# Four graph layers on 32 graphs: two issuing queues for the first adjacency matrix, and another order of all steps

## The chip, the cores and the metric

The kernel runs on one core of a Trainium2 chip. The metric is the device time of one launch, in microseconds (us). Three runs of the kernel before gave a median of 2910.88 us (2910.64 to 2910.99).

A core has engines that run side by side, each on its own instruction queue: TensorE (PE in the profile; its weight loads are PEld), VectorE (DVE), ScalarE (ACT), GpSimd (POOL) and SyncE (SP). Transfers are issued from the queues of SP, ACT and POOL.

## The reference

The inputs are x (32 graphs, 512 nodes, 256 features), adj (32, 512, 512) and a node mask, all in float32 but for the mask. Four layers follow each other; each is `x = layernorm(x + layer(x))`:

- Layer 0: `h = (1 + eps) x + adj @ x`, then `relu(h @ W1 + b1) @ W2 + b2`, with a hidden width of 512.
- Layer 1: graph attention with 4 heads: `e = leaky_relu(e_dst + e_src)` where `adj > 0.5`, softmax, times `x @ W`, plus a bias.
- Layer 2: attention with 8 heads of width 32: `softmax(q k' / sqrt(32) + log(adj + 1e-6)) v`, then an output projection with a bias.
- Layer 3: attention with one head: `softmax(mask((x W x') * adj)) x`.

## The kernel before

The graphs are independent. One graph is cut into several hundred steps by `graph(g)`; `prepare()` makes the steps for the weights. A step (`Step`) has a name, an engine, a planned duration, the steps it needs, the buffers it takes, and the instructions that it issues. Nodes come in 4 chunks of 128 partitions, features in 2.

Names of steps and lines that matter below:

- `la0i` to `la3i` (L670) issue the loads of the four 256 KB strips of a graph's adjacency matrix; `lxi` (L677) issues the load of x (512 KB). `at0` to `at3` (L695) transpose the strips on TensorE, `atd` (L701, DVE) and `ate` (L705, ACT) copy them out of PSUM, and `h0`, `h1` (L728) multiply x with the result into hT. `f` (L751) and `y` (L770) are the two dense products of layer 0.
- Layer 1: `v1` (L819), the row R that is sent through DRAM and broadcast, the elements `z` (L922 ACT, L933 DVE), products `o1` (L956), the sums `d1` (L993).
- Layer 2: `q`, `k` (L1078), `v2` (L1096), scores `s0` to `s7` (L1115), exponentials (L1128 ACT), the product with adj (L1137 DVE), values `n0` to `n7` (L1173), row sums `d2` (L1220), which GpSimd's adding transfers prepare (L1148, L1201), and the projection `p` (L1299).
- Layer 3: `i` (L1343), `t` (L1357), transposes `u` (L1396), `w` (L1411).
- Preparation: loads of eps, b1, the biases and two attention vectors go out on ACT's queue, the larger weights on SP's (all L348). `fmax`, `fm`, `fmt` (L530) and `fmb` (L540) find a bound on the scores.

TensorE works in four arrangements of its array. Most products use all of it. Scores use four tiles of 32 rows at a time (mode `row`), the values of layer 2 and all row sums use tiles of 32 columns (`c32`), those of layer 1 two tiles of 64 columns (`c64`).

The order in which the steps of all graphs are issued is worked out when the kernel is built, by `Plan.order`: it keeps a clock for each engine, takes the steps that could start within `ahead` of the earliest one, and issues the one with the lowest due time. A due time is made of the graph's turn times `period`, less the longest way from the step to the end of its graph, plus an offset for the step's name, plus `stay` times the price of a change of TensorE's arrangement:

```python
due = turn[g] * period - self.left[g][name] + moved[name] + stay * change
```

The prices stand in a table, `CHANGE`: 0.1 from the whole array to `row` or `c32`, 0.218 from `row` to anything else but itself, 0.13 from `c32` to the whole array, 0.12 from `c32` to `row`. The offsets `moved` come from a list of names and from disturbances that a random generator makes from seeds (`shifts`). `rush` moves the turns of the last three graphs forward. At most 6 graphs are open at once (`window`). All of this only sets the order in the queues; on the chip each instruction waits for what it needs.

Of the kernel before, what the change touches and what calls it, by code (L numbers as in the profile page):

```python
# [17 lines left out]
P = 128  # L18
# [28 lines left out]
class Plan:  # L47
# [31 lines left out]
    def step(self, name, eng, us, after=(), take=(), free=(), mode=""):  # L79


        def add(emit):
            steps = self.steps[-1]
            known = {**steps, **{f"^{n}": s for n, s in self.steps[0].items()}}
            assert name not in steps and all(a in known for a in after), (name, after)
            takes = []
            for b in take:
                kind, _, key = b.partition("=")
                key, _, rest = key.partition("/")
                takes.append((kind, key or kind, int(rest or 0)))  # L90
# [137 lines left out]
def fast_path(  # L228
# [23 lines left out]
    nc = tc.nc  # L252
# [47 lines left out]
    def blk(i):  # L300
# [257 lines left out]
    def graph(g):  # L560
# [3 lines left out]
        t = {"g": g}  # L564
# [7 lines left out]
        def strip(key, shape, name):  # L572
            return sb.tile(shape, F32, tag=f"D{slot[key]}", name=f"{name}_{g}")
# [88 lines left out]
        for c in range(NC):  # L662

            @step(
                f"la{c}i", "sp", 0.45, (f"la{c-1}i",) if c else (),
                take=(f"D=A0{c}/5",) if c else ("live", "L0", "D=A00/8"),
            )
            def _(c=c):
                t[f"A{c}"] = strip(f"A0{c}", [P, N], f"A{c}")
                nc.sync.dma_start(t[f"A{c}"], adj[g].rearrange("(c p) m -> p c m", p=P)[:, c, :])  # L670

            transfer(f"la{c}", 1.0 if g == 0 else 2.0, (f"la{c}i",), land=4.0 if g else 2.0)

# [1257 lines left out]
```

## Time and profile before

| | |
|---|---|
| median of three runs | 2910.88 us |
| the profiled execution: its time | 2910.6 us |
| its span, first to last instruction | 2908.8 us |
| mean granted TensorE clock | 0.998 |
| TensorE busy (15521 matmuls) | 2878.8 us, 99% |
| TensorE weight loads busy | 1655.2 us, 57% |
| DVE / ACT / POOL busy | 2256.4 / 1903.9 / 454.9 us |
| DMA, mean over the span | 148 GB/s |

The page gives the busy time of each engine and the chain of work that ended last. A line of a group or of the timeline names the kernel's line, the engine, the operation, the tiles written and read, and the shape; `32*128` is the part of the array in use (rows by columns). A line of the waits says which engine waited at which line for whom: in total, how often, and the longest. In the timeline the first two numbers are the start and the length in us, and what stands in brackets is the idle time ahead of it and what ended it.

### The profile page before, as it was taken

What the parts mean: (1) busy time and instruction counts of PE and PEld (TensorE: products, weight loads), DVE (VectorE), ACT (ScalarE), POOL (GpSimd) and SP (SyncE); (2) the same over time, 40 slices, a digit from 0 to 9 for tenths busy, and PEclk for the clock granted to TensorE, in tenths of its full rate; (3) what the DMA queues carried; (4) which work ended last, traced back from release to release, by engine and by line L of the source; (5) the groups of instructions that cost most, each with busy time, mean ns of one, the idle gap of its engine ahead of it and who ended that gap; (6) DMA issues with size and microseconds to landing.
All of it is one profiled execution on the core that took longest, in us unless ns stands there. A gap on an engine that the chain in (4) does not pass through costs nothing.

```text
span 2908.8 us, 42662 instructions
## 1 busy us (share of the span) xinstructions
PE 2878.8 (99%) x15521; PEld 1655.2 (57%) x15521; DVE 2256.4 (78%) x4389; ACT 1903.9 (65%) x3818; POOL 454.9 (16%) x494
## 2 busy tenths in 40 slices
PE   8989999999999999999999999999999999999998
PEld 6645555556555566555565555665555655556445
DVE  2786788777888777887778887778877788887975
ACT  3676666776656766667766567666667665676754
POOL 1111111111111111111111111111111111111110
PEclk9999999999999999999999999999999999999999
DMA  6367775567866567765678665677656786665851
GB/s 186 70 153 150 159 170 135 137 145 167 186 142 139 134 160 174 165 141 137 140 165 187 145 138 134 159 172 165 145 138 137 163 187 147 138 144 126 183 120 41
DMA packets 134879, 430.70 MB, mean 148 GB/s; under 512 B 13628, under 2 KB 53384, under 8 KB 102792
## 3 DMA queue, kind: packets, MB, share of 16 engines
q0 software_dynamic: 45568, 277.89, 49.2%
q1 hardware_dynamic: 88112, 149.75, 15.4%
q8 instruction: 125, 2.05, 0.3%
q14 instruction: 90, 0.74, 0.1%
q10 hardware_dynamic: 984, 0.28, 0.1%
HBM read 183.25 MB, written 17.08 MB: 69 GB/s over the span
## 4 chain that ended last, share of the span: by engine, by line
PE 95%; DMA 2%; ACT 1%; DVE 1%; issue 0%; POOL 0%; POOLq 0%; ACTq 0%; SPq 0%
PE s L1115 9%; PE o_ps L1173 8%; PE hT_ps L728 8%; PE o_ps L1411 8%; PE s L1357 8%; PE y_ps L770 8%; PE o_ps L956 7%; PE h1T_ps L751 7%; PE iT_ps L1343 4%; PE v_ps L819 4%; PE o2p_ps L1299 4%; PE kT_ps L1078 4%; PE qT_ps L1078 4%; PE v_ps L1096 4%; PE xT_t L1059 2%; PE eT_t L1396 2%
## 5 line engine op out<-in xcount | busy, mean ns | idle before, releaser
L1128 ACT ACTIVATE z<-s 128x512 f32<-128x512 f32 x1024 | 558.9, 609 | 131.4 <-PE s L1115 101.6
L1137 DVE SCALAR_TENSOR_TENSOR z<-AT,z 128x1024 f32<-128x1024 f32 x512 | 603.0, 1207 | 36.4 <-ACT z L1128 36.0
L933 DVE SCALAR_TENSOR_TENSOR z<-z,T,edge 128x512 f32<-128x512 f32 x512 | 363.7, 747 | 157.7 <-ACT z L922 156.9
L922 ACT ACTIVATE z<-R_bc,nT,S 128x512 f32<-128x512 f32 x512 | 395.5, 819 | 8.4 <-PE y_ps L770 3.0
L641 ACT ACTIVATE x<-x,shift,rstd 128x256 f32<-128x256 f32 x508 | 296.1, 609 | 152.0 <-DVE shift L631 152.0
L1148 POOL DMA_DIRECT2D z<-z x186 | 166.8, 903 | 1029.4 <-DVE nmax L1379 254.5
L623 POOL TENSOR_TENSOR rstd<-ve,nhalf 128x4 f32<-128x4 f32 (+1 forms) x131 | 153.5, 1172 | 978.2 <-DVE ve L617 953.8
L1115 PE MATMUL s<-qT,kT 32*128 32x512 f32 x2048 | 287.4, 633 | 1.0 <-ACT kT L1084 1.0
L1173 PE MATMUL o_ps<-z,v 128*32 128x512 f32 x2048 | 267.4, 602 | 1.8 <-DVE z L1137 1.7
L956 PE MATMUL o_ps<-z,v 128*64 128x512 f32 x1024 | 240.5, 601 | 2.1 <-DVE y L1028 2.1
L983 DVE TENSOR_TENSOR z<-z 128x1024 f32<-128x1024 f32 (+1 forms) x256 | 231.4, 952 | 13.0 <-PE o_ps L956 12.9
L1411 PE MATMUL o_ps<-x,eT 128*128 128x256 f32 x1024 | 239.3, 382 | 0.7 <-ACT eT L1401 0.7
L751 PE MATMUL h1T_ps<-hT,w_sb 128*128 128x512 f32 x512 | 230.4, 593 | 0.0
L1357 PE MATMUL s<-xT,iT 128*128 128x512 f32 x512 | 226.6, 594 | 0.7 <-ACT z L1128 0.7
L770 PE MATMUL y_ps<-w_sb,h1T 128*128 128x256 f32 x1024 | 226.7, 379 | 0.0
L1263 DVE RECIPROCAL rdT<-rdT 128x256 f32<-128x256 f32 x128 | 219.1, 1731 | 2.1 <-ACT rdT L1256 2.0
L600 DVE BATCH_NORM_STATS2 st<-x 128x6 f32<-128x256 f32 x508 | 211.0, 415 | 7.5
L1411 PEld LDWEIGHTS o_ps<-x,eT 128*128 128x128 f32 x1024 | 187.5, 190 | 46.3 <-ACT z L1387 21.0
L728 PE MATMUL hT_ps<-AT,x 128*128 128x384 f32 (+2 forms) x768 | 210.2, 383 | 0.0
L770 PEld LDWEIGHTS y_ps<-w_sb,h1T 128*128 128x128 f32 x1024 | 194.1, 190 | 27.9 <-issue 0.8
L1115 PEld LDWEIGHTS s<-qT,kT 32*128 32x128 f32 x2048 | 86.0, 183 | 166.0 <-ACT z L1128 118.8
L825 ACT COPY v<-v_ps 128x264 f32<-128x264 f32 x128 | 47.9, 376 | 183.7 <-PE v_ps L819 183.2
(155 smaller groups left out, 4241.3 us busy)
## 6 DMA issues: line engine op xcount, KB each, us to landing
z<-z POOLq DMA_DIRECT2D x186, 1024.0 KB, 8.5
A<-in_adj_dram SPq DMA_DIRECT2D x256, 256.0 KB
x<-biases POOLq DMA_DIRECT2D x96, 512.0 KB, 7.1
R_bc<-R_dram SPq DMA_DIRECT2D x32, 1024.0 KB
z<-z POOLq DMA_DIRECT2D x62, 512.0 KB, 8.7
x<-in_x_dram SPq DMA_DIRECT2D x32, 512.0 KB
out_dram<-x SPq DMA_DIRECT2D x31, 512.0 KB
nm<-in_nodemask_dram SPq DMA_DIRECT2D x32, 256.0 KB
```

The source lines that it names most:

```text
L728: nc.tensor.matmul(ph[:, cols], t["x"][:, m, blk(d)], moving, start=(k == 0), stop=(k == len(parts) - 1),)
L751: nc.tensor.matmul(ph, w1_sb[:, d, blk(f)], t["hT"][:, d, :], start=(d == 0), stop=(d == DC - 1))
L770: nc.tensor.matmul(py[:, j, :], t["h1T"][:, f, blk(2 * c2 + j)], w2_sb[:, f, :], start=(f == 0), stop=(f == HC - 1),)
L922: nc.scalar.activation(t[f"e{h}"][:, c, :], t["Rbc"][:, h, :], AF.Relu, bias=t["nT"][:, h, c : c + 1], scale=t["S"][:, h, c : c + 1],)
L933: nc.vector.scalar_tensor_tensor(z, z, t["T"][:, h, c : c + 1], t["edge"][:, c, :], op0=ALU.add, op1=ALU.mult)
L956: nc.tensor.matmul(po[j * F1 : (j + 1) * F1, :], t["v"][:, c, h * F1 : (h + 1) * F1], t[f"e{h}"][:, c, :], start=(c == 0), stop=(c == NC - 1),
L1115: nc.tensor.matmul(pk, t["k"][hs, o, blk(c)], t["q"][hs, o, :], start=True, stop=True)
L1128: nc.scalar.activation(t[f"E{k}"][:, j, :], t[f"ps{k}{j}"], AF.Exp, scale=QSCALE)
L1137: nc.vector.scalar_tensor_tensor(z, t["AT"][:, c, None, :].to_broadcast([P, 2, N]), ADJ_EPS, z, op0=ALU.add, op1=ALU.mult,)
L1173: nc.tensor.matmul(t[f"n{o}"][32 * j : 32 * j + 32, :], t["v2"][:, c, o * P + F2 * j : o * P + F2 * (j + 1)], t[f"E{k}"][:, j, :], start=( ...
L1357: nc.tensor.matmul(pt, t["iT"][:, d, blk(c)], t["xT3"][:, d, :], start=(d == 0), stop=(d == DC - 1),)
L1411: nc.tensor.matmul(py, t[f"eT{c}"][:, blk(m)], t["x"][:, m, :], start=(m == 0), stop=(m == NC - 1),)
```

## The change

For graph 0 alone, the loads of strips 1 and 3 are issued by ACT's queue, those of strips 0 and 2 by SP's as before. And the arguments of the plan are others: `stay` is 80 where it was 165, there are 14 seeds of disturbances where there were 8 (the first two are the same), the last three turns are moved by 1.7, 1.0 and 0.0 where it was 2.0, 1.1 and 0.1, and nearly all of the some 320 offsets of step names are different. The planner itself, the steps and what each step computes stay as they are.

```diff
             @step(
-                f"la{c}i", "sp", 0.45, (f"la{c-1}i",) if c else (),
+                f"la{c}i", "act" if g == 0 and c % 2 else "sp", 0.45, (f"la{c-1}i",) if c else (),
                 take=(f"D=A0{c}/5",) if c else ("live", "L0", "D=A00/8"),
             )
             def _(c=c):
                 t[f"A{c}"] = strip(f"A0{c}", [P, N], f"A{c}")
-                nc.sync.dma_start(t[f"A{c}"], adj[g].rearrange("(c p) m -> p c m", p=P)[:, c, :])
+
+                (nc.scalar if g == 0 and c % 2 else nc.sync).dma_start(
+                    t[f"A{c}"], adj[g].rearrange("(c p) m -> p c m", p=P)[:, c, :]
+                )
...
     with tc.manual_schedule():
-        plan.run([(24, 0.1, 6, 165.0, ((959604, 5.0), (114893, 5.0), (451585, 5.0), (104136, 2.0), (561761, 2.0), (241046, 2.0), (593942, 2.0), (984585, 2.0)), (2.0, 1.1, 0.1), (('R', 0.5), ('Re', -5.0),
...
-('la0.q', -74.0), ('la0i', -35.5), ('la1.q', -166.5), ('la1i', -58.5), ('la2.q', -21.5), ('la2i', 3.0), ('la3.q', -48.0), ('la3i', 4.0),
...
-('lx.q', -17.5), ('lxi', 9.0),
...
+        plan.run([(24, 0.1, 6, 80.0, ((959604, 5.0), (114893, 5.0), (428442, 5.0), (827982, 2.0), (379309, 5.0), (168251, 5.0), (904211, 5.0), (197558, 5.0), (201498, 2.0), (728276, 2.0), (358280, 2.0), (281265, 2.0), (22270, 2.0), (235352, 2.0)), (1.7, 1.0, 0.0), (('R', -7.5), ('Re', 3.0),
...
+('la0.q', 6.0), ('la0i', -1.0), ('la1.q', 9.0), ('la1i', 55.5), ('la2.q', -7.0), ('la3.q', 10.0), ('la3i', -2.0),
...
+('lx.q', 1.5), ('lxi', 2.0),
...
```

More of the change, by code (lines that the diff above doesn't have):

```diff
@@ L1458, in fast_path @@
     with tc.manual_schedule():
-        plan.run([(24, 0.1, 6, 165.0, ((959604, 5.0), (114893, 5.0), (451585, 5.0), (104136, 2.0), (561761, 2.0), (241046, 2.0), (593942, 2.0), (984585, 2.0)), (2.0, 1.1, 0.1), (('R', 0.5), ('Re', -5.0), ('Rl.q', 20.0), ('Rli', -15.0), ('Rs.q', 3.0), ('Rsi', 6.5), ('Rt', -62.0), ('ST', -37.5), ('ab', 6.0), ('as00', 6.5), ('as01', 6.0), ('as10', 0.5), ('as11', -1.0), ('as20', -27.0), ('as30', -86.5), ('as31', -18.5), ('at0', 3.0), ('at1', 2.0), ('at2', 9.5), ('at3', 6.0), ('atd0', -20.0), ('atd1', 0.5), ('atd2', -30.0), ('atd3', -21.0), ('ate0', 6.5), ('ate1', -13.0), ('ate2', 16.5), ('ate3', 19.0), ('cd1', 29.5), ('cd2', 17.0), ('cd3', 1.0), ('cd5', 39.5), ('cd6', 15.0), ('cd7', 33.5), ('cq1', -4.0), ('cq2', -78.0), ('cq3', 15.0), ('cq5', -20.0), ('cq6', -20.5), ('cq7', 2.0), ('d1', -25.0), ('de', 9.5), ('dev1.0', 27.0), ('dev2.0', 24.5), ('dev3.0', 12.5), ('dev4.0', 55.0), ('dt', 5.5), ('e00', 7.0), ('e01', -4.0), ('e02', 7.0), ('e03', 18.0), ('e10', 3.5), ('e11', 68.5), ('e12', -4.0), ('e13', 7.5), ('e20', 11.0), ('e21', -9.0), ('e22', 3.0), ('e23', -7.5), ('e30', -4.0), ('e31', -8.0), ('e32', 15.0), ('e33', 34.5), ('e40', -1.0), ('e41', -6.5), ('e42', 7.0), ('e43', -41.0), ('e50', 3.0), ('e51', 11.5), ('e52', 30.5), ('e53', 55.5), ('e60', 2.0), ('e61', -31.5), ('e62', 22.0), ('e63', 7.5), ('e70', 5.0), ('e71', 42.0), ('e72', 8.5), ('ed0', 32.0), ('ed1', -5.0), ('ed2', 72.0), ('f0', 19.0), ('f2', -0.5), ('f3', 8.0), ('fd0', 35.5), ('fd1', 41.0), ('fe0', -14.5), ('fe1', -1.0), ('fe2', -8.0), ('fe3', -4.0), ('fq0', -10.5), ('fq1', -10.0), ('h0', 19.0), ('h1', -8.0), ('he0', 2.5), ('he1', -14.0), ('hsb.q', 37.5), ('hsl', 7.0), ('i0', 6.0), ('i1', 7.0), ('ie0', -3.5), ('ie1', -1.0), ('k0', 2.0), ('k1', 18.5), ('ke0', 63.0), ('ke1', 2.0), ('la0.q', -74.0), ('la0i', -35.5), ('la1.q', -166.5), ('la1i', -58.5), ('la2.q', -21.5), ('la2i', 3.0), ('la3.q', -48.0), ('la3i', 4.0), ('lb0.q', -17.5), ('lb0i', -18.5), ('lb1.q', -2.0), ('lb1i', -15.5), ('lb2i', 6.0), ('lb3.q', -40.5), ('lb3i', -20.5), ('ldn.q', -0.5), ('ldni', 3.0), ('lx.q', -17.5), ('lxi', 9.0), ('m00', 2.5), ('m01', 9.0), ('m10', -16.0), ('m11', 12.5), ('m20', 6.5), ('m21', 0.5), ('m30', 4.5), ('m31', -4.5), ('m40', 13.0), ('m41', -31.5), ('m60', -24.0), ('m61', 42.5), ('m70', -1.0), ('m71', 19.5), ('n0', -2.0), ('n1', -31.0), ('n2', -6.5), ('n3', 6.0), ('n4', -3.5), ('n5', -12.0), ('n6', -12.5), ('n7', 32.5), ('nd0', 17.0), ('nd1', 32.0), ('no0', 0.5), ('no1', 9.5), ('node', 27.5), ('o100', 1.0), ('o101', 5.5), ('o110', 6.0), ('o111', 7.0), ('oe0', 23.5), ('oe1', 11.5), ('out0.q', 3.0), ('p0', 35.5), ('p1', 10.5), ('q0', 1.5), ('q1', -87.5), ('qe0', -27.0), ('qe1', -14.0), ('r10', 2.5), ('r11', 7.0), ('r12', 13.0), ('r13', -22.0), ('r20', 87.0), ('r21', 2.0), ('r22', -12.0), ('r23', 10.0), ('r30', 99.5), ('r31', -41.0), ('r33', 24.5), ('r40', -2.0), ('r41', -8.0), ('r42', -66.5), ('r43', 53.5), ('rc00', 5.0), ('rc10', 6.0), ('rc11', 6.5), ('rd1', -21.5), ('rd30', -68.5), ('rd31', 15.0), ('rd32', -5.5), ('rd33', -67.5), ('s0', 4.0), ('s1', -6.5), ('s2', -9.5), ('s3', -41.5), ('s4', -18.5), ('s5', -17.0), ('s6', -18.0), ('s7', -42.0), ('sh1.0', -1.0), ('sh2.0', 92.5), ('sh3.0', 59.0), ('sh4.0', -0.5), ('st10', -13.5), ('st11', 5.0), ('st12', -1.5), ('st13', 40.5), ('st20', -15.5), ('st21', 139.0), ('st22', 13.0), ('st23', 55.5), ('st30', 6.5), ('st31', 36.0), ('st32', 24.0), ('st33', -2.5), ('st40', -22.0), ('st41', 26.0), ('st42', -3.5), ('st43', 96.0), ('t0', 10.5), ('t1', -1.0), ('t2', -14.5), ('t3', -8.5), ('ta0', 27.0), ('ta1', 15.0), ('ta2', -3.5), ('ta3', -2.0), ('tb0', 4.5), ('tb1', -5.5), ('tb2', 4.0), ('tb3', -29.0), ('te0', -17.0), ('te1', -19.5), ('te2', 26.0), ('te3', -3.5), ('u0', -0.5), ('u1', -26.0), ('u2', 6.5), ('u3', 1.0), ('ue0', 17.0), ('ue1', 26.5), ('ue2', 30.5), ('ue3', -1.0), ('v10', 9.5), ('v11', -37.5), ('v12', 2.5), ('v13', -11.5), ('v20', 2.0), ('v21', -1.0), ('v22', -5.0), ('v23', 2.0), ('va1.0', 6.0), ('va2.0', 9.5), ('va3.0', 9.0), ('va4.0', 34.5), ('ve10', -5.5), ('ve11', -25.0), ('ve12', 9.5), ('ve13', -25.5), ('ve20', -1.5), ('ve21', 14.5), ('ve22', -6.0), ('ve23', -6.0), ('w0', 9.0), ('w1', 5.0), ('w2', 9.5), ('w3', -4.0), ('wx0', -29.5), ('wx2', 2.0), ('wx3', 21.5), ('x10', 1.0), ('x11', 1.0), ('x30', 1.0), ('x31', -10.0), ('xd1', -14.5), ('xd2', -5.0), ('xd3', -0.5), ('xe10', 4.0), ('xe11', -0.5), ('xe20', -3.0), ('xe21', -19.0), ('xe30', -23.5), ('xq1', -16.5), ('xq3', -45.0), ('xsi', -6.0), ('xt10', -46.5), ('xt11', -4.0), ('xt20', -6.0), ('xt30', -6.5), ('xt31', -5.5), ('y0', 9.5), ('y1', -4.0), ('yd00', -12.0), ('yd01', 59.5), ('yd10', 11.5), ('yd11', 88.0), ('yn0', -131.5), ('yn1', 9.0), ('yn2', -131.5), ('yn3', 17.5), ('yt0', 9.0), ('yt1', -21.5), ('yt2', -16.0), ('yt3', -18.0), ('z00', 13.5), ('z02', 104.5), ('z03', -3.0), ('z10', -4.5), ('z11', 12.0), ('z12', 3.0), ('z13', -2.0), ('z20', 22.0), ('z22', -11.5), ('z23', -6.5), ('z30', -2.0), ('z31', -39.0), ('z32', 21.5), ('z33', -7.0), ('zm00', -27.5), ('zm01', 56.5), ('zm10', -8.0), ('zm11', 21.5), ('zm20', 8.5), ('zm21', 0.5), ('zm30', 3.0), ('zm31', 28.5)))])
@@ new lines, in fast_path @@
+        plan.run([(24, 0.1, 6, 80.0, ((959604, 5.0), (114893, 5.0), (428442, 5.0), (827982, 2.0), (379309, 5.0), (168251, 5.0), (904211, 5.0), (197558, 5.0), (201498, 2.0), (728276, 2.0), (358280, 2.0), (281265, 2.0), (22270, 2.0), (235352, 2.0)), (1.7, 1.0, 0.0), (('R', -7.5), ('Re', 3.0), ('Rl.q', 1.0), ('Rli', -7.5), ('Rs.q', 12.5), ('Rsi', 40.0), ('Rt', -85.5), ('ST', -44.5), ('ab', 2.5), ('as00', -32.5), ('as01', -17.5), ('as10', -14.0), ('as11', -59.0), ('as20', -108.0), ('as21', -47.0), ('as30', -159.5), ('as31', -27.5), ('at0', -10.5), ('at1', -19.0), ('at2', -36.5), ('atd0', -28.5), ('atd1', -43.0), ('atd2', -17.5), ('atd3', -3.5), ('ate0', 22.5), ('ate1', 6.5), ('ate2', -9.5), ('ate3', 1.0), ('cd1', -3.5), ('cd2', -8.0), ('cd3', 13.5), ('cd5', -5.5), ('cd6', 2.5), ('cd7', 9.0), ('cq1', 47.5), ('cq2', 37.0), ('cq5', 34.0), ('cq6', -0.5), ('cq7', 24.5), ('d1', -79.5), ('d2', -2.0), ('de', -47.0), ('dev2.0', 5.5), ('dev3.0', -8.0), ('dev4.0', 19.5), ('dt', 7.0), ('e00', 7.0), ('e01', -6.0), ('e02', 36.5), ('e03', -22.5), ('e10', 5.0), ('e11', -18.0), ('e12', -15.5), ('e13', 11.0), ('e20', -37.0), ('e21', -14.5), ('e22', -0.5), ('e23', 48.5), ('e30', -6.0), ('e31', -1.5), ('e32', 7.5), ('e40', 2.0), ('e42', 5.0), ('e43', 2.0), ('e50', 1.0), ('e51', 7.0), ('e52', -5.0), ('e53', 0.5), ('e60', 24.0), ('e61', -9.5), ('e62', 1.0), ('e63', -3.0), ('e70', -4.0), ('e71', -3.0), ('e72', 8.0), ('e73', 4.0), ('ed0', 69.5), ('ed1', -14.5), ('ed2', -0.5), ('ed3', -5.5), ('f0', 36.5), ('f1', -11.0), ('f3', 2.0), ('fd0', 7.0), ('fd1', 6.0), ('fe0', -41.0), ('fe1', 11.0), ('fe2', -10.0), ('fe3', 3.0), ('fq0', 19.0), ('fq1', -19.5), ('h0', 15.0), ('h1', 4.5), ('he0', 7.0), ('he1', -0.5), ('hsb.q', 10.5), ('hsbi', -9.0), ('hsl', 1.0), ('i0', 5.5), ('i1', -29.0), ('ie0', 1.5), ('ie1', 10.0), ('k1', -2.5), ('ke0', 4.0), ('ke1', 47.5), ('la0.q', 6.0), ('la0i', -1.0), ('la1.q', 9.0), ('la1i', 55.5), ('la2.q', -7.0), ('la3.q', 10.0), ('la3i', -2.0), ('lb0.q', 2.5), ('lb0i', 10.5), ('lb1.q', -11.5), ('lb1i', 43.0), ('lb2.q', 50.0), ('lb2i', -5.0), ('lb3.q', -2.0), ('lb3i', 27.0), ('ldn.q', 19.5), ('ldni', 9.0), ('lx.q', 1.5), ('lxi', 2.0), ('m00', -11.0), ('m01', 2.0), ('m10', 26.5), ('m21', -22.5), ('m30', 1.5), ('m31', 12.5), ('m40', 14.0), ('m41', 12.5), ('m50', -14.0), ('m51', 3.0), ('m61', 52.5), ('m70', -5.0), ('m71', -2.5), ('n0', 19.0), ('n1', 8.0), ('n2', 6.5), ('n3', 12.5), ('n4', -6.0), ('n5', -8.5), ('n6', 3.0), ('n7', 1.0), ('nd0', -29.0), ('nd1', -25.5), ('no0', 23.5), ('no1', 10.0), ('node', -2.5), ('o100', 8.5), ('o101', -11.0), ('o110', 26.0), ('o111', 2.5), ('oe0', 5.5), ('oe1', 42.5), ('out0.q', 5.0), ('p0', 26.0), ('p1', 12.0), ('q0', -1.0), ('q1', 4.5), ('qe0', 9.0), ('qe1', -49.0), ('r10', -16.0), ('r11', -7.5), ('r12', 9.0), ('r13', 2.5), ('r20', 10.0), ('r21', -9.0), ('r22', 1.0), ('r23', 63.0), ('r30', 74.0), ('r31', -2.0), ('r32', 7.5), ('r33', 10.5), ('r40', 9.5), ('r41', 1.0), ('r42', 21.0), ('r43', 13.5), ('rc00', 10.0), ('rc01', -30.5), ('rc10', 30.0), ('rc11', -10.0), ('rd30', -34.5), ('rd31', 19.0), ('rd32', 2.5), ('rd33', -11.0), ('s0', 2.5), ('s1', 15.0), ('s4', -29.0), ('s5', -31.5), ('s6', -42.0), ('s7', -46.0), ('sh1.0', 0.5), ('sh2.0', 96.0), ('sh3.0', -10.0), ('sh4.0', 8.0), ('st10', 16.0), ('st11', 6.5), ('st12', 7.0), ('st13', 4.0), ('st20', -28.0), ('st21', 171.5), ('st22', 7.5), ('st23', 119.0), ('st30', 13.5), ('st31', 4.5), ('st32', 7.0), ('st40', 24.0), ('st41', -23.5), ('st42', 13.5), ('st43', -2.0), ('t0', 9.5), ('t1', -3.0), ('t2', 5.0), ('t3', 0.5), ('ta0', 46.0), ('ta1', 2.5), ('ta2', -14.0), ('ta3', -39.0), ('tb0', -7.0), ('tb1', -18.0), ('tb3', -28.5), ('te0', 1.0), ('te1', 6.5), ('te2', 12.0), ('te3', -1.0), ('u0', 18.0), ('u1', 8.0), ('u2', -39.0), ('u3', -18.0), ('ue0', -3.0), ('ue1', 3.0), ('ue2', 10.5), ('ue3', 1.0), ('v10', -11.5), ('v11', -26.5), ('v12', -7.0), ('v20', -1.5), ('v21', -18.0), ('v22', -12.5), ('v23', 1.0), ('va1.0', -1.0), ('va2.0', -5.0), ('va3.0', 22.5), ('va4.0', 16.0), ('ve10', -25.0), ('ve11', 2.0), ('ve12', 3.0), ('ve13', -5.0), ('ve20', 9.0), ('ve21', -2.0), ('ve22', 20.5), ('ve23', 7.0), ('w0', -5.5), ('w1', -1.0), ('w2', -7.0), ('w3', 11.0), ('wx0', -36.0), ('wx1', 3.5), ('wx2', -4.0), ('wx3', 8.0), ('x10', -21.0), ('x11', 13.5), ('x30', 19.5), ('x31', 2.0), ('xd1', -17.5), ('xd3', -1.0), ('xe10', -7.0), ('xe11', -1.0), ('xe20', -26.0), ('xe21', -2.0), ('xe30', -3.0), ('xe31', 4.0), ('xq1', -7.0), ('xq2', 61.5), ('xq3', 4.0), ('xs.q', 13.0), ('xt11', 13.5), ('xt21', -5.0), ('xt30', 1.0), ('xt31', -31.0), ('y0', 13.0), ('y1', -15.5), ('yd00', -3.5), ('yd01', 60.0), ('yd10', 30.0), ('yd11', 95.0), ('yn0', -150.5), ('yn1', -10.0), ('yn2', -241.0), ('yt0', 11.5), ('yt1', 0.5), ('yt2', -3.0), ('yt3', 12.0), ('z00', 23.0), ('z01', 34.0), ('z02', 60.0), ('z03', -7.0), ('z10', 2.5), ('z11', 8.0), ('z12', -21.0), ('z13', -42.0), ('z20', 21.0), ('z21', -3.0), ('z23', 0.5), ('z30', 3.0), ('z31', 6.0), ('z32', 43.0), ('z33', -2.5), ('zm00', -3.0), ('zm01', 109.5), ('zm10', 36.5), ('zm20', 44.5), ('zm21', -19.0), ('zm30', 1.0), ('zm31', 52.0)))])
```

## The prediction

> **What bounds the kernel now.** I read the page's busy times and its chain first, then the waits of TensorE, then TensorE's instructions in order of time for one graph in the middle, then the first 14 us.
>
> ```profile
> PE 2878.8 (99%) x15521; PEld 1655.2 (57%) x15521; DVE 2256.4 (78%) x4389; ACT 1903.9 (65%) x3818; POOL 454.9 (16%) x494
> PE 95%; DMA 2%; ACT 1%; DVE 1%; issue 0%; POOL 0%; POOLq 0%; ACTq 0%; SPq 0%
> ```
>
> TensorE is busy for 99% of the span and carries 95% of the chain that ended last. So only three things can move the time: the matmuls themselves (unchanged), what lies between them inside "busy" time, and TensorE's few idle stretches. The waits of TensorE alone:
>
> ```profile
> PE AT_t L695 <- DMA A<-in_adj_dram: 4.9, 1, 4.9
> PE hT_ps L728 <- DMA x<-in_x_dram: 4.5, 1, 4.5
> PE o_ps L956 <- DVE y L1028: 2.1, 1, 2.1
> PE o_ps L1173 <- DVE z L1137: 1.7, 4, 0.6
> PE fmb L540 <- DVE fm L535: 1.1, 1, 1.1
> ```
>
> Two are the first strips and the first x (9.4 us); the others are between 100 and 280 us. From 322 to 2371 us TensorE waits 0.2 us in all: every graph there takes 88.81 us, start of hT to start of hT. What a longer search can still find there is inside the busy time. One stretch of that period:
>
> ```profile
> 1089.83 1.14 PE L1115 MATMUL s<-qT,kT 32*128 32x512 f32 x8
> 1090.90 1.98 PE L1343 MATMUL iT_ps<-xT,w_sb 128*128 128x512 f32 x4
> 1092.82 1.14 PE L1115 MATMUL s<-qT,kT 32*128 32x512 f32 x8
> 1093.89 1.06 PE L1173 MATMUL o_ps<-z,v 128*32 128x512 f32 x8
> 1094.88 1.14 PE L1115 MATMUL s<-qT,kT 32*128 32x512 f32 x8
> ...
> 1100.87 7.03 PE L1357 MATMUL s<-xT,iT 128*128 128x512 f32 x16
> 1107.73 0.27 PE L1010 MATMUL d_t<-ident,dT 128*128 128x128 f32 x1
> ```
>
> Sixteen full-array matmuls take 1107.73-1100.87 = 6.86 us, 0.429 each. Four of iT should take 1.72 and take 1.92 before a tiling of another kind follows: +0.20. Eight score matmuls, four at a time in the 32-row tiling, should take 2x0.429 = 0.86 and take 1.07: +0.21. Eight of the 32-column tiling take 0.99: +0.13; the 64-column form gives +0.15 in the same way. I call a stretch in one tiling a run. The period has 22: 5 full-array, 7 of scores, 7 of 32 columns, 3 of 64. They cost 5x0.19 + 7x0.21 + 7x0.14 + 3x0.15 + 0.16 (a change inside the 32-column kind) = 4.0 us of 88.81; the matmuls alone need 84.8.
>
> Summed over the trace this way: 2734 us of matmuls, 125 us at the ends of 726 runs, 25.6 us of further stalls (20.8 of them between 100 and 280 us, where the pipeline fills), 4.9+9.0 us at the start, 0.8 in the last run and 9.9 after the last matmul: 2909, the span of 2908.8.
>
> **What the Trainium skill says.** "TensorEngine Tiling (Array Packing)", Key Properties: a change of tiling mode drains TensorE. The trace agrees: each change costs 0.13 to 0.21 us and inside a run there is nothing. "TensorE: Matmul & The Clock Gate", What's actually happening: after an idle window of some 3.4 us the array's clock falls to half. The trace agrees at 198 to 201.3 us, where the granted clock is 0.50 after the idle around fmt and fmb; eight matmuls lose about 1.7 us there. "DMA: Bandwidth & Descriptors", Issuing engines are not separate DMA queues: issuing from two engines saves only issue time. The trace bounds that: SP's four strip issues take 1.82 us.
>
> **The change, part by part.**
>
> *Strips 1 and 3 of graph 0 go from SP to ACT.* This removes 2 issues from SP, at 1.82/4 = 0.45 us each: 0.9 us. It adds 2 to ACT, whose own load issues take 0.33 to 1.19 us (median 0.42): 0.84 us. The start is bound by x, not by strips:
>
> ```profile
> 4.93 3.65 PE L695 MATMUL AT_t<-ident,A 128*128 128x128 f32 x16 [4.93 <-DMA A<-in_adj_dram]
> 5.88 0.37 SPq L677 DMA_DIRECT2D x<-in_x_dram  x1
> 13.04 0.77 PE L728 MATMUL hT_ps<-ATd,x 128*128 128x128 f32 x2 [4.47 <-DMA x<-in_x_dram]
> ```
>
> TensorE has transposed all strips at 8.58 and waits for x until 13.04. SP issues x only at 5.88, after w1 at 4.98, and both issues waited for earlier small loads (eps, b1) to land: the tenth and twelfth load wait for the second and fourth, so eight loads at most are in flight. If x takes the place that strip 1 leaves, it goes out near 1.2 us. Its 7.0 us from issue to landing then end at 8.2, and the bound passes to the strips. The new offsets work against them: la1i gets +55.5. Adding up the planner's durations, its due time without that is some 10 us before b1, 17 before the bias loads and 29 before a0 and a1, so +55.5 puts strip 1 behind all seven small loads on ACT. Those end at 7.1 in this trace. With 4.1 us from issue to landing (the first strip: 0.76 to 4.90), strips 1 and 3 land at about 11.3 and 11.7; 0.44 for a transpose and 0.54 for its copy give a first hT at 12.7. Best case (strips early, x at 8.2, copies at 8.4 to 11.1 moved up by 1): hT at 10, -3 us. Worst (ACT's eighth place waits for a landing that is itself late): +3. I take -1. Behind the two issues on ACT stand the table load (1.28) and the four AT copies (2.7 us), which end at 11.1 with 1.9 us to spare; without that cover the 0.84 us goes onto the start.
>
> *A new order for every step.* No computing instruction is added or removed; each queue is reordered, the loads on SP and the 344 adding transfers on POOL too. Three terms follow.
>
> Periodic part: from 322.2 to 2370.8 us are 23.07 periods. One pair of runs fewer per graph (scores and 32-column) saves 0.21+0.14 = 0.35 us, or 8.1 us; one more costs the same, or 0.41x23.07 = 9.5 where a full-array run is cut. Which way it goes can't be read from the list. The price of changes is weighted less (stay 165 becomes 80: leaving scores for the full array, priced 0.218, delays a due time by 17 us where it was 36), which speaks for more runs. For fewer speaks the room: 7 runs hold 8 score steps, and a pair of score steps already stands together once in the period. The planner sees this cost nearly right: its prices for the same period sum to 85.1+3.3 = 88.5 us against 88.81 measured. An order that is shorter for it should be shorter on TensorE. I take 20 runs per graph: -8.1. Bounds: 18 runs, -16; 24 runs, +9.5.
>
> What hides the reordering elsewhere is the slack of the other engines in a period: ACT 59 of 88.8 us busy, DVE 70, POOL 14, DMA engines 0.66. If that cover goes, a late DVE product appears as a TensorE wait. The largest seen after the start is 2.1 us; once per graph that would be 48 us, so I do not take the cover as certain.
>
> Filling, 100 to 280 us: stalls of 20.8 us over 58 runs, ended by DVE products, by the fmax-fm-fmb chain of the preparation, and by x normalised late. They happen once, and both orders meet the same latencies. Removing all gives -20.8; another bad crossing, say the 4.5 us around fmt and fmb again, +4.5. I take a tenth: -2.1.
>
> Draining: the last three graphs' due times are moved forward by 1.7, 1.0 and 0 times 24 us in place of 2.0, 1.1 and 0.1. Stalls there are 4.3 us, and 9.9 us lie after the last matmul. Between -4 and +4; I take 0.
>
> Sum: -1 - 8.1 - 2.1 + 0 = -11.2. Span 2908.8 - 11.2 = 2897.6; the profiled run was 2910.6, 1.8 outside the span, and the median is 0.3 above that: **2899.7 us**.
>
> **The rivals.**
> - *The orders are worth the same.* 22 runs again, the filling as before. For it: in the middle, the trace has nothing left but those 4.0 us a graph. Against it: 22 is far above the 14 or so that pairs of score and value steps would allow. With -1 at the start: 2910.
> - *Slower: more changes of tiling.* In the periodic part, the lighter price lets one more full-array step cut a score stretch per graph: 24 runs, +9.5, less 1 at the start: 2919. It decides from 0.25 us per graph on (5.8/23.07), less than one pair. For it: 165 to 80. Against: the planner still counts each change.
> - *Strip 1 comes late behind ACT's small loads.* The start loses 3 us and doesn't gain 1: 2903.7. For it: the +55.5 offset and the eight loads in flight. Against: x's own wait hides most of it. This is also the case in which the two queues don't do what they are for.
> - *A large gain.* 18 runs (-16.2) and half of the filling's stalls (-10.4), start -1: 2883.3. For it: 20.8 us of stalls stand in the trace. Against: they follow from few graphs being open.
>
> **How the numbers follow.** A measurement of this kernel can tell 0.2% (5.8 us) from no change. Forecast 0.38, large gain 0.13, late strip 0.05 (all faster by over 0.2%: 0.56); same 0.22; more changes 0.22. The range 2881 to 2920 takes in both ends of the run count and leaves out some 0.15, a worse start or broken cover above, a filling nearly free of stalls below. The likeliest case alone: 2893 to 2905.
>
> **What would show it.** Right: hT to hT near 88.46 us in the middle with 20 runs, hardly any TensorE wait there; fewer waits from 100 to 280 us; first hT at 12 us, no longer ended by x. Wrong: a period over 88.81, a TensorE wait that recurs each graph (DVE z or ACT xT), or a first hT after 13. If the period is as it was and the time is not, the ends decide, and my weights were misplaced.

## The result, and the profile after

The changed kernel takes 3039.1 us (median of four runs, 3031.3 to 3043.3) against 2910.9: a ratio of 1.0436, 95% interval 1.0414 to 1.0458. It is slower by 128 us, where 11 us less were forecast and 2920 was the upper end of the range.

From the page after, its busy times and its chain, by engine and by line:

```profile
PE 2915.9 (96%) x15521; PEld 1681.9 (55%) x15521; DVE 2239.7 (74%) x4389; ACT 1921.8 (63%) x3818; POOL 453.2 (15%) x494
PE 73%; DMA 18%; ACT 4%; DVE 3%; issue 1%; SPq 0%; POOL 0%; ACTq 0%; POOLq 0%; DVEq 0%
DMA R_dram<-R_rows 9%; PE s L1118 8%; PE s L1360 8%; PE o_ps L959 7%; PE o_ps L1176 7%; DMA R_bc<-R_dram 6%; PE y_ps L773 6%; PE kT_ps L1081 4%; PE iT_ps L1346 4%; PE v_ps L822 4%; PE h1T_ps L754 3%; PE o_ps L1414 3%; PE qT_ps L1081 3%; PE v_ps L1099 3%; PE hT_ps L731 2%; PE o2p_ps L1302 2%
```

Transfers carry 18% of the chain, where it was 2%, and two names that hardly stood on it before are among its longest: the 8 KB write of layer 1's row R to DRAM (9%), and its 1 MB broadcast load (6%). (The change shifts line numbers by 3.) The waits of TensorE:

```profile
PE kT_ps L1081 <- ACT xT L1066: 73.7, 18, 7.2
PE AT_t L698 <- DMA A<-in_adj_dram: 15.3, 3, 8.2
PE xT_t L1062 <- ACT x L641: 9.1, 19, 2.0
```

The first is a wait that the kernel before hardly had (0.4 us in all): k of layer 2 waits for a copy of xT by ACT, in 18 graphs, 4.1 us each. The time from the start of one graph's R transpose to the next shows where the 127.3 us of span come from. From graph 6 to graph 27 (21 periods) it was 88.81 us each before and is 93.61 on average now: +100.8. Up to graph 6 the kernel loses 15.1, after graph 27 it loses 11.4.

Periods without that wait take 88.56 us. They have 19 runs (stretches in one tiling) where there were 22, so the new order is better where the planner looked. One period with the wait, in the timeline of the changed kernel (SP's, GpSimd's and ACT's lines, and TensorE's wait):

```profile
1159.46 3.04 SPq L1330 DMA_DIRECT2D A<-in_adj_dram  x4
1161.33 0.86 POOL L1151 DMA_DIRECT2D z<-z  x1 [7.03 <-DVE z L1376]
1163.29 0.85 POOL L1151 DMA_DIRECT2D z<-z  x1 [1.09 <-ACT z L1390]
1163.82 1.17 POOL L1204 DMA_DIRECT2D z<-z  x1
1168.61 0.32 SPq L870 DMA_DIRECT2D R_dram<-R_rows  x1
...
1182.18 0.34 SPq L877 DMA_DIRECT2D R_bc<-R_dram  x1
1193.55 1.52 ACT L925 ACTIVATE z<-R_bc,nT,S 128x512 f32<-128x512 f32 x2 [12.33 <-DMA R_bc<-R_dram]
1194.97 1.05 ACT L1066 COPY xT<-xT_t 128x512 f32<-128x512 f32 x2
1195.59 3.78 PE L1081 MATMUL kT_ps<-xT,wkT 128*128 128x512 f32 x4 [4.37 <-ACT xT L1066]
```

Read it upwards. TensorE waits 4.4 us for xT. The two xT copies stand behind two z steps on ACT's queue, and ACT has waited 12.3 us for R_bc. R_bc could be issued only when R's own write had landed, 13.6 us after it went out. In the kernel before, the same place:

```profile
1199.30 2.79 SPq L1327 DMA_DIRECT2D A<-in_adj_dram  x3
1203.25 0.86 POOL L1148 DMA_DIRECT2D z<-z  x1 [10.58 <-DVE nmax L1379]
1203.79 1.17 POOL L1201 DMA_DIRECT2D z<-z  x1
1204.97 0.92 POOL L1148 DMA_DIRECT2D z<-z  x1
1209.25 1.99 SPq L867 DMA_DIRECT2D R_dram<-R_rows  x1
...
1217.65 0.34 SPq L874 DMA_DIRECT2D R_bc<-R_dram  x1
```

There the last strip of layer 3's adjacency matrix goes out before GpSimd's three adding transfers, and R's write lands in 8.4 us. In the changed order, the first adding transfer gets in ahead of the last strips. What the queues moved in the 4 us after R's write, first the changed kernel (1168.6 to 1172.6 us), then the one before (1209.25 to 1213.25):

```profile
q0 software_dynamic: 103, 0.76, 91.4%
q1 hardware_dynamic: 104, 0.19, 14.4%
```

```profile
q0 software_dynamic: 112, 0.77, 103.4%
```

q0 is GpSimd's queue, q1 that of SP. Before, nothing of q1 moved in these 4 us, not even R's own write; no strip was left ahead of it. Now q1 still holds strips, and they drain at 0.19 MB in 4 us beside the adding transfers' 0.76. The packet counts are equal, 103 and 104. This is as the Trainium skill has it in "DMA: Bandwidth & Descriptors", Queues, rings and completion order: each DMA engine goes round between the queues packet by packet. With packets of 7.4 KB on average on one side and 1.8 KB on the other, equal turns give the strips a fifth of the bytes. R's write stands behind them.

Over graphs 6 to 27, R's write to the issue of its load takes 8.2 us before and 13.1 now, and the first z after that load comes 16.2 us and 22.6 us after the write. ACT's wait for R_bc, from 497.8 to 2370 us, first before and then now:

```profile
ACT z L922 <- DMA R_bc<-R_dram: 0.7, 1, 0.7
ACT z L925 <- DMA R_bc<-R_dram: 202.9, 20, 13.9
```

Most of the waits also cost clock: at 15 of the 18, those of 2.4 us and more, TensorE's granted clock is 0.50 for 3.4 or 6.8 us, beginning during the wait or within 1.4 us after it. After the wait above, from the windows view (the third number from the end is the clock):

```profile
1195.60:1199.00 3.40, 3.40 (x4) 1.49 (x5) 2.17 (x8) 3.40 (x6) 0.00 (x0) 0.50 1.10 226
```

Four matmuls of kT take 3.78 us there, 1.88 without a wait ahead of them.

### The profile page after: what moved, and what is told of

It is laid out like the page before. It is cut to its first block, busy times and chain, and to the rows that moved or that the text cites. A ratio compares the mean times of both kernels' runs of the same rounds, so it can differ in the third digit from the quotient of the medians.

```text
span 3036.1 us, 42696 instructions
## 1 busy us (share of the span) xinstructions
PE 2915.9 (96%) x15521; PEld 1681.9 (55%) x15521; DVE 2239.7 (74%) x4389; ACT 1921.8 (63%) x3818; POOL 453.2 (15%) x494
## 4 chain that ended last, share of the span: by engine, by line
PE 73%; DMA 18%; ACT 4%; DVE 3%; issue 1%; SPq 0%; POOL 0%; ACTq 0%; POOLq 0%; DVEq 0%
DMA R_dram<-R_rows 9%; PE s L1118 8%; PE s L1360 8%; PE o_ps L959 7%; PE o_ps L1176 7%; DMA R_bc<-R_dram 6%; PE y_ps L773 6%; PE kT_ps L1081 4%; PE iT_ps L1346 4%; PE v_ps L822 4%; PE h1T_ps L754 3%; PE o_ps L1414 3%; PE qT_ps L1081 3%; PE v_ps L1099 3%; PE hT_ps L731 2%; PE o2p_ps L1302 2%
## 5 line engine op out<-in xcount | busy, mean ns | idle before, releaser
L1131 ACT ACTIVATE z<-s 128x512 f32<-128x512 f32 x1024 | 540.0, 610 | 97.2 <-PE s L1118 93.1
L925 ACT ACTIVATE z<-R_bc,nT,S 128x512 f32<-128x512 f32 x512 | 402.9, 818 | 248.9 <-DMA R_bc<-R_dram 245.2
L641 ACT ACTIVATE x<-x,shift,rstd 128x256 f32<-128x256 f32 x508 | 290.0, 614 | 161.3 <-DVE shift L631 161.3
L1176 PE MATMUL o_ps<-z,v 128*32 128x512 f32 x2048 | 259.0, 602 | 2.0 <-DVE z L1140 1.9
L1360 PE MATMUL s<-xT,iT 128*128 128x512 f32 x512 | 244.4, 605 | 0.0
L754 PE MATMUL h1T_ps<-hT,w_sb 128*128 128x512 f32 x512 | 238.4, 609 | 1.9 <-ACT hT L738 1.9
L986 DVE TENSOR_TENSOR z<-z 128x512 f32<-128x512 f32 (+1 forms) x256 | 231.1, 952 | 4.6 <-PE o_ps L959 4.6
L1081 PE MATMUL kT_ps<-xT,wkT 128*128 128x512 f32 x256 | 146.2, 700 | 74.1 <-ACT xT L1066 73.7
L902 DVE CUSTOM_DVE_ANT_0 xs_row<-xs_row,wgT 128x256 f32<-128x256 f32 x64 | 27.2, 425 | 216.0 <-DMA xs_row<-xs_dram 214.9
## 6 DMA issues: line engine op xcount, KB each, us to landing
z<-z POOLq DMA_DIRECT2D x62, 512.0 KB, 10.6
```

Of the source, the lines that this page charges most:

```text
L754: nc.tensor.matmul(ph, w1_sb[:, d, blk(f)], t["hT"][:, d, :], start=(d == 0), stop=(d == DC - 1))
L925: nc.scalar.activation(t[f"e{h}"][:, c, :], t["Rbc"][:, h, :], AF.Relu, bias=t["nT"][:, h, c : c + 1], scale=t["S"][:, h, c : c + 1],)
L1081: nc.tensor.matmul(pq, wT[n][:, d, blk(o)], t["xT2"][:, d, :], start=(d == 0), stop=(d == DC - 1))
L1131: nc.scalar.activation(t[f"E{k}"][:, j, :], t[f"ps{k}{j}"], AF.Exp, scale=QSCALE)
L1176: nc.tensor.matmul(t[f"n{o}"][32 * j : 32 * j + 32, :], t["v2"][:, c, o * P + F2 * j : o * P + F2 * (j + 1)], t[f"E{k}"][:, j, :], start=( ...
L1360: nc.tensor.matmul(pt, t["iT"][:, d, blk(c)], t["xT3"][:, d, :], start=(d == 0), stop=(d == DC - 1),)
```

## The experiments

Two parts were taken alone first. The theory: the loss is R's late round trip, which ACT's queue hands on to TensorE. Rivals: the start with its two queues; ACT's new order by itself; the adding transfers slowing every transfer alike. Each ratio is against runs of the kernel before that were made beside it (medians 2911.5 to 2912.0 us).

**The two queues alone.** The kernel before, in its order:

```diff
-                nc.sync.dma_start(t[f"A{c}"], adj[g]...)
+                (nc.scalar if g == 0 and c % 2 else nc.sync).dma_start(t[f"A{c}"], adj[g]...)
```

> The kernel before, in its own order, with strips 1 and 3 of graph 0 issued by ACT at the places that the order before gives them (strip 1 right after eps). Theory: the first part of the change is small by itself. The first hT waits for x, and x now goes out up to 0.9 us earlier: 2908 to 2912 us. Rival (the two queues are what costs): over 2920 us.

Measured: 2913.7 us, ratio 1.0005 (0.9996 to 1.0014), no difference that can be told, though just over the expected range. First hT came later and not earlier, at 14.1 us and not 13.0: x no longer ends the wait, strip 3 does. It went out on ACT at 9.1 us, behind bias loads.

**The order alone.** The changed kernel with all strips on SP:

```diff
-                f"la{c}i", "act" if g == 0 and c % 2 else "sp", 0.45, ...
+                f"la{c}i", "sp", 0.45, ...
```

> The changed kernel's order with all strips of graph 0 on SP again. Theory: the loss comes from the repeated stalls of the middle, so nearly all of it stays: 3025 to 3040 us, with the first hT some us earlier than 19.3. Rival (the start costs most): below 2950 us.

Measured: 3028.7 us, ratio 1.0386 (1.0339 to 1.0433). First hT at 15.5 us, TensorE's wait for xT 71.0 us in 17 graphs. The order makes nearly all of the loss; ACT's share in the strips adds some 4 us at the start.

**R's load without R's write.**

```diff
-                t["Rbc"].rearrange("p h n -> p (h n)"), row_bcast(t["Rdram"], H1 * N)
+                t["Rbc"].rearrange("p h n -> p (h n)"), row_bcast(biases.rearrange("k c d -> k (c d)")[0:1, :], H1 * N)
```

> The changed kernel, with the broadcast row R read from a DRAM row that is written once at the start, so that its load needn't wait for the landing of R's own 8 KB write (layer 1's R is left out of the result; all instructions stay). Theory (the round trip of R is late, ACT waits for it with the xT copies behind): ACT's wait for R_bc and TensorE's wait for xT go from 74 us to under 10, the middle period becomes 88.6 us: 2915 to 2935 us. Rival (ACT's order alone makes xT late): 3020 us or more.

Measured: 2922.6 us. The wait for xT no longer stands among TensorE's waits, and the middle takes 88.61 us on average. ACT's own order, with z ahead of xT, is the same in this run: it does no harm when R comes in time. ACT still waits for R_bc here, 96.3 us in 21 graphs, and the first z starts 17.1 us after R's write; that much TensorE bears.

**R's write from another queue.** The result stays whole here:

```diff
-            nc.sync.dma_start(t["Rdram"], t["Rr"][: H1 * NC, :])
+            nc.scalar.dma_start(t["Rdram"], t["Rr"][: H1 * NC, :])
```

> The changed kernel, with R's 8 KB write issued by ACT's queue in place of SP's, nothing else moved. Theory (the write stands in SP's ring behind strips that are still draining beside the adding transfers): from Rs to the issue of R_bc it takes 3 to 5 us and not 12.9, the stalls of xT shrink to under 15 us in all: 2915 to 2945 us. Rival (the adding transfers slow every transfer, whichever ring it is in): still 10 us or more, and over 3000 us.

Measured: 2925.5 us, ratio 1.0043 (1.0029 to 1.0057). Write to load takes 5.6 us on average (3 to 5 were expected), and z starts 16.3 us after the write, against 16.2 in the kernel before. TensorE's wait for xT in this run:

```profile
PE kT_ps L1081 <- ACT xT L1066: 1.6, 2, 1.4
```

One word in one line takes back 114 of the 128 us. The adding transfers run as in the changed kernel, so the rival that they alone make R this late is out: most of the lateness comes from standing behind the strips in SP's queue. They are not without effect. R's write took 8.2 us in the kernel before, with no strip ahead of it in the window shown above, and ACT still waits 92.3 us for R_bc in this run. The prediction took over that a second issuing engine saves only issue time; here a second queue saved 114 us, because what stood ahead of the write was left behind.

**Smaller adding transfers.** The changed kernel with a quarter of each row:

```diff
-  src, dst = (t[f"E{b}"].rearrange("p h n -> p (h n)") for b in (k, a))
+  src, dst = (t[f"E{b}"].rearrange("p h n -> p (h n)")[:, :N] for b in (k, a))
```

> The changed kernel, with GpSimd's adding transfers of the row sums cut to a quarter of each row (three quarters of the sums of layer 2 are left out; the same number of transfers). Theory (the strips drain slowly because of the adding transfers, and R behind them): Rs to R_bc takes under 5 us, hardly a stall of xT: 2910 to 2930 us. Rival (R is late by its own latency or by SP's order): still over 10 us, over 3000 us.

Measured: 2908.8 us, just below the expected range; middle 88.56 us, write to load 3.7 us, and ACT's wait for R_bc is gone. So both must come together for the loss: strips still queued ahead of R (without them, in the kernel before, 8.2 us and no loss), and adding transfers that take most of the engines' time beside them. What wasn't run is the new order with the last strips ahead of the adding transfers again.

**z behind the copies on ACT.** The changed kernel; in `run`, the order `out` is edited before its steps are issued (`xe20` and `xe21` are the two xT copies):

```diff
+        for g in range(6, 28):
+            i = max(k for k, e in enumerate(out) if e[0] == g - 1 and e[1] in ("xe20", "xe21"))
+            late = [e for e in out[:i] if e[0] == g and len(e[1]) == 3 and e[1][0] == "z"]
+            if [e[1] for e in late] != ["z10", "z30"]:
+                continue
+            out = [e for e in out[: i + 1] if e not in late] + late + out[i + 1 :]
```

> The changed kernel, with the first two z steps (z10, z30) of each graph in the middle moved behind the two xT copies on ACT's queue; R comes as late as before. Theory (ACT's queue carries R's lateness to TensorE): TensorE's wait for xT, 74 us, is gone, but the copies of h1T stand behind z31 and wait in its place, so a good part comes back there: 2950 to 3020 us. Rival (xT is late for another reason): no change, 3030 us or more.

Measured: 3058.9 us (two runs), no faster than the changed kernel. The waits of TensorE there:

```profile
PE kT_ps L1088 <- ACT xT L1073: 39.8, 10, 6.9
PE xT_t L1069 <- ACT x L648: 36.7, 35, 2.9
...
PE y_ps L780 <- ACT h1T L767: 8.0, 8, 1.3
```

The edit took hold in 13 of the 22 graphs. In the other nine, two stretches in the middle, four z steps stand ahead of xT, and the code leaves them alone. In the 13, TensorE's wait for xT is gone; the 39.8 us come from graphs that were not edited. But the 13 are no faster, 94.2 us per period where the same graphs took 93.6: waits for other ACT work take its place, for normalised x (up to 2.9 us) and h1T. By its time the run falls into the rival's range (3030 us or more); the waits speak against the rival, as xT is on time once no z stands ahead of it. That ACT carries the lateness is borne out; my size was not. Moving one consumer past a late producer moved the stall to the next one.

**A late R in the kernel before.** Twice written, and then three times, in its own order. The edit for two writes (`once` is another DRAM tile):

```diff
+            nc.sync.dma_start(once, t["Rr"][: H1 * NC, :])
-            nc.sync.dma_start(t["Rdram"], t["Rr"][: H1 * NC, :])
+            nc.sync.dma_start(t["Rdram"], once)
```

> The kernel before, with R's row written to DRAM twice in turn (first to another DRAM tile, then copied from there), so that its round trip is 4 to 8 us longer; the rest as before. Theory (both orders leave R a margin of 1 to 2 us, and the one before only happens to stay within it): the period rises by 2 to 6 us and the same waits for xT or h1T appear: 2960 to 3040 us. Rival (the order before tolerates a late R, the new order is what is fragile): 2911 to 2920 us.

Measured: 2924.1 us; z starts 18.0 us after the first write, 1.8 later than before, and the period rises by 0.08 us only. The expectation missed: two writes came to less than I had reckoned, and 1.8 us is still within what TensorE bears; the time falls between the ranges of theory and rival. Of the 11 us of span lost here, 6.2 are after graph 27.

> The kernel before, with R's row written three times in turn, so that z starts 21 to 22 us after the first write and not 16.2 (18.0 with two writes, where the period rose by 0.1 us only). Theory (both orders have the same shape there, and only the lateness of R tells them apart): the period rises by 3 to 5 us, with TensorE waiting for xT: 2990 to 3030 us. Rival (the order before tolerates a late R, which is why it was fast): under 2950 us.

Measured: 3131.1 us (two runs), ratio 1.0753 (1.0733 to 1.0774). z starts 24.7 us after the first write (I had reckoned with 21 to 22), and the period is 96.87 us, so the loss is larger than expected. From the waits of TensorE:

```profile
PE kT_ps L1082 <- ACT xT L1067: 137.8, 27, 8.1
```

The same instruction waits for the same copy. The order before shows no sign of being more robust than the new one: it bears 1.8 us of lateness, and at 8.5 us it loses 8.1 per graph. The loss per graph goes with the start of z after the write, whichever order it is: in the order before 16.2 us, no loss; 18.0, 0.1 us; 24.7, 8.1; in the new order, over its 88.56 us, 16.3 and 17.1, 0.05 us; 22.6, 5.05.

**The start.** Since strip 1 came late, three versions of the kernel before put graph 0's loads first. Strips 0 and 2 and x on SP, strips 1 and 3 first on ACT:

> The kernel before, with the four strips and x of graph 0 ahead of all other loads: strips 0 and 2 and then x on SP, strips 1 and 3 first on ACT. Theory (two queues help only if nothing stands ahead of the strips): first hT at 9 to 11 us and not 13.0, TensorE's waits at the start 5 us shorter: 2905 to 2909 us. Rival (the loads' bandwidth sets the start): first hT at 12 to 13 us, 2911 us.

Measured: 2911.9 us, ratio 1.0001 (0.9992 to 1.0010), the rival's number. The first hT matmul is at 8.6 us: x is early. But the AT copies stand on ACT behind loads of biases and vectors that wait to be issued, and TensorE stops again until 14.0 us. Then these loads behind the AT copies:

> The kernel before, with the strips and x of graph 0 first as in the run before it, and the loads of the biases and attention vectors behind the four AT copies on ACT's queue. Theory (in that run x had landed by 8.6 us, and only the AT copies, which stood behind waiting load issues on ACT, kept TensorE idle until 14.0): the whole hT runs from about 9 us, 4 to 5 us earlier than before: 2905 to 2908 us. Rival (another load, w1 or the biases, then comes late and takes it back): 2910 to 2914 us.

Measured: 2911.6 us, ratio 0.9999 (0.9991 to 1.0008). First hT at 10.6 us. Now the 0.5 KB load of eps, third on ACT, lands only at 9.1 us; the ATd additions need it and the copies wait for those. Then eps first:

> As the run that put the strips and x of graph 0 first and the loads of the biases and attention vectors behind the AT copies, but with eps as ACT's first load again. Theory (there the small eps load had slipped behind the strips, the ATd additions waited for it until 9.5 us, and the AT copies for those): the AT copies start at about 5.5 us, hT when x lands at 8 to 10 us: 2906 to 2909 us. Rival (the start of the kernel is worth nothing because a later wait takes it up): 2910 to 2913 us.

Measured: 2910.5 us against 2911.6, ratio 0.9998 (0.9990 to 1.0006). First hT at 8.9 us, 4.2 earlier than before; but graph 1's hT starts only 1.4 us earlier and the span is 1.0 us shorter, as the rival said. In this order the start can be won and is then given back within the filling, so the two queues are worth nothing there that can be measured.

**Both mended.** The new order, R's write on ACT, and the start with eps behind the strips:

> The changed kernel's order, with R's write on ACT and the start of x10. Theory: the middle keeps its 88.56 us, the start wins about 10 us against the run with R on ACT alone, filling and draining stay worse than before by some 13 us: 2912 to 2918 us. Rival (with both mended the new order shows the gain that it was forecast): 2900 to 2906 us.

Measured: 2917.3 us, ratio 1.0022 (1.0010 to 1.0033). The middle averages 88.65 us, a gain of 3.3 us over 21 periods. Up to graph 6 it is 0.6 us behind the kernel before, and after graph 27 it loses 7.6 us. No version that computes the whole result was found that beats the kernel before.

## Why the prediction was wrong

**The bound** was read rightly: TensorE's order and its waits decide.

**Periodic part.** The direction was right and the size close: 20 runs and 88.46 us were forecast, 19 runs and 88.56 us came in the undisturbed periods. The 23.07 periods would have given -5.8 us, not -8.1. That they are so close is partly luck: it wasn't a pair of scores and 32 columns that went. The 7 runs of scores and the 5 full-array ones are all there; two of 32 columns and one of 64 went. By the prediction's own prices that is 2x0.14 + 0.15 = 0.43 us a graph, and it was 0.25. Against the lighter price of changes I put the planner's own interest, and that held. The rival with more changes of tiling was wrong in its sign.

**The step that failed** is the one on what hides the reordering. I listed the other engines' busy shares as its cover, wrote that the cover was not certain, priced a recurring wait of 2.1 us at 48 us for the run, and then left that out of the sum and of the rivals; a broken cover was put among the 0.15 outside the range. It measured 93.61 - 88.56 = 5.05 us per period, 106 us in 21 periods. The kind of the slack was mistaken: the cover wasn't ACT's free time but the lead of one small transfer over its first reader. The profile before showed it, in SP's waits from 367 to 2370 us:

```profile
SPq L874 <- DMA R_dram<-R_rows: 144.8, 22, 8.3
```

SP waits there for R's write in every graph, 6.6 us each, and z is reached 16.2 us after the write, shortly after R_bc has landed. I had named the queues that are reordered, and costed none of their transfers. In the list of what would show the prediction wrong, "a TensorE wait that recurs each graph (DVE z or ACT xT)" is what came.

**The planner as evidence.** I took it that an order shorter for the planner is shorter on TensorE, because its prices of tiling changes fit. For the period before they do (88.5 us against 88.81). But it lets SP's loads and GpSimd's adding transfers run on separate queues, `q1` and `qa`, which don't slow each other, with a fixed landing of 5.0 us for R's write (the `land` of `transfer("Rs", ...)`), where the runs show 3.7 to 13.1 us, by what else is in the queues. To such a model it costs nothing to let an adding transfer get in ahead of the last strips. That the new order came about in this way is my reading of the code; no run shows it.

**The start.** -1 was forecast, with +3 at worst. Measured: first hT at 19.3 us, +6.3. The rival of the late strip came true, with twice its size. Strip 1 did come behind the seven small loads, as reckoned, but these didn't end at 7.1. From the trace of the changed kernel (SPq and ACTq are the issues of loads on these queues):

```profile
1.21 0.42 SPq L680 DMA_DIRECT2D x<-in_x_dram  x1
8.12 0.34 ACTq L348 DMA_DIRECT2D a<-in_L_gnn_a_src_dram  x1
9.34 0.40 ACTq L671 DMA_DIRECT2D A<-in_adj_dram  x1
12.38 0.33 ACTq L671 DMA_DIRECT2D A<-in_adj_dram  x1
14.24 1.12 PE L698 MATMUL AT_t<-ident,A 128*128 128x128 f32 x4 [8.18 <-DMA A<-in_adj_dram]
```

x went out at 1.21, as I had said it could. But the eleventh load, a0, waits for the third, and that is the small load of b1. Issued together with x, it landed at 8.1 us, where it had landed at 5.9; x landed at 7.9. So a0 stood until 8.12, strip 1 went out at 9.34, when w1 had landed, and strip 3 at 12.38, when a1 had. I had seen that eight loads at most are in flight and not applied it to the new sequence. The two queues by themselves cost nothing measurable (1.0005). In the new order, with its +55.5, ACT's share moves the first hT from 15.5 to 19.3 us; the offset alone was not run.

**Filling and draining.** Forecast -2.1 and 0. With R mended (its write on ACT) the kernel is 10.8 us behind at graph 6, and 6.1 behind at the first hT. With the start mended too it is 0.6 behind at graph 6, where the order before with the same start is 0.4 behind. So nearly all of the 10.8 goes back to the start, and the new order's filling is worth about 0, where -2.1 was forecast. After graph 27 the run with R mended loses 8.2. TensorE waits 9.9 us there, 1.6 in the kernel before; the longest wait, 4.3 us, is h1T's for ACT's copy of hT, and the clock is 0.50 for 3.4 us from there on. What makes that copy late stays open.

**The range.** It was built from the run count and the ends, so nothing in it could reach 3039. The rival on the other side was a small one; the large one was in my own text as a condition.

**A reading of the clock.** At 198 us the trace shows the half clock that the prediction names, but not an idle window of 3.4 us ahead of it: from 193 to 198 us TensorE is idle for 2.4 us in all, at most 1.1 at a time. In the changed kernel a wait of 2.4 us was enough, and one of 1.8 was not.

## What to carry to other kernels

When TensorE is full and steps are only reordered, cost the new order by its round trips: for each small transfer whose reader is near the head of an in-order queue, note the lead before, what stands ahead of it in its own queue, and who is behind the reader. Then ask what a loss of that lead costs per graph, and put that into the range. An order found on a model is no better than the model's weakest term; here that was a landing time that depends on the other queues, entered as a constant.

## What the runs showed that was not expected

- An 8 KB write took 3.7, 5.6, 8.2 or 13.1 us until the load that needed it was issued: with small adding transfers, alone on ACT's queue, in the order before, behind strips in SP's queue.
- Two queues with packets of unlike size shared the DMA engines by packets, 103 to 104, not by bytes, 0.76 to 0.19 MB.
- Starting the first hT 4.2 us earlier was worth 1.0 us of span.
